# Self attention with exponentials summed on VectorE, products with ones a head group later, the next layernorm beside the maxima, and the query bias scaled later

## The chip, the cores and the metric

The kernel runs on one core of one Trainium2 chip. The core has five engines that run their own instruction queues side by side and wait for each other through semaphores: TensorE (PE in the profile, with its weight loads shown apart as PEld), VectorE (DVE), ScalarE (ACT), GpSimd (POOL) and SyncE (SP, which here only issues transfers). SBUF is the working memory of 128 partitions; PSUM takes what TensorE writes. The metric is the device time of one execution in microseconds (us). The time before is 848.01 us, the median of three runs (848.0 to 848.03).

## The reference

One decoder layer in float32 over four sequences (batches) of 512 tokens with 512 channels: self attention with 16 heads of 32 channels, cross attention against a given context, and a feed-forward part. Each begins with a layernorm and is added to x.

```python
x = x + attn(layernorm(x), q_w, q_b, k_w, k_b, v_w, v_b, o_w, o_b)   # causal, 16 heads of 32
x = x + xattn(layernorm(x), ctx, ctx)                                 # causal, 16 heads, masked by -10000
x = x + ffn(layernorm(x), W_up, W_down, W_gate, W_expert)

def attn(x, ...):
    q, k, v = x @ q_w.T + q_b, x @ k_w.T + k_b, x @ v_w.T + v_b      # split into heads
    scores = where(causal, einsum('bhqd,bhkd->bhqk', q, k) * 32 ** -0.5, -inf)
    ctx = einsum('bhqk,bhkd->bhqd', softmax(scores), v)
    return ctx @ o_w.T + o_b
```

What matters here is the softmax of the self attention: for every query, the largest score, the exponentials, their sum over the keys, and the quotient of the weighted values by that sum.

## The kernel before

**Stages.** Each of the four batches goes through the same stages (L781 to L824). with_maxima (L726) computes the scores with queries on the partitions and takes their largest values; between its matmuls it lays other matmuls as filler (query, key and value projections in the first batch, the feed-forward of the batch before later). attend (L753) computes the scores again with keys on the partitions, subtracts the maxima, takes exponentials and multiplies with the values. out_projection (L577) follows with the residual and the next layernorm; then the cross attention goes through the same two stages, and then the feed-forward. A group g is four heads on 128 partitions, so there are NC = 4 groups in a batch.

**Order.** The order of the instructions on PE, DVE, ACT and POOL is the order of the program text (manual_schedule, L773); SP's transfers are ordered by the framework. Every engine takes its queue in order, so an instruction that waits holds up everything behind it.

**PSUM.** All of PSUM is one pool of four buffers, each a pair of 512-column banks (pair, L65). A score unit takes two pairs (heads 0 and 1, heads 2 and 3), a group's value products one (pv: the numerators in half 0, the denominators in half 1).

**Attention stage, in steps.** attend goes through 12 units: for each group key block 0 (512 queries), key block 1 (384), and key blocks 2 and 3 together (256 and 128).
- scores (L360): eight matmul records per key block for the scores (L370; a float32 product is two records), then a bf16 product with ones that adds the negative maximum (L381). Two ScalarE exponentials (L394), each over a pair of heads, write pt in SBUF; two GpSimd selects (L396) set the masked corner to zero. pt lies in work buffers with the tags pt0, pt1 and pt2, two of each.
- values (L409) of a unit comes two units later: for u = 0 the products of pt with the values, for u = 1 those of pt with a matrix of ones (L418), which sum the exponentials over the keys and put the denominators into the second half of pv.
- divide (L429), after a group's last unit: VectorE transposes the denominators in 32x32 blocks (L438), takes the reciprocal of one column of each block (L440), transposes it back spread out (L441), and multiplies the numerators (L449) into oT, the tile that out_projection reads.
- The next batch's first layernorm (layernorms, L188, in five steps) is handed to attend as sides (L790) and runs on VectorE and GpSimd after every second unit; each of its first four steps also issues a transfer of 128 rows of x into xin (L466), which has two buffers. Its transposes (turns) run in out_projection.

**Maxima stage.** maxima (L267) takes per unit two pairs, two ScalarE copies into SBUF (L292), two GpSimd selects (L298) and VectorE reductions (L310). split (L323) makes three bf16 parts of a group's maxima, and rows (L334) transposes them on TensorE some units later.

**Start.** bqs_sb, the query bias times 1/sqrt(32), is made by a GpSimd instruction in the section of constants (L125). GpSimd's part in the layernorm, variance plus epsilon (L201) and its power -1/2 (L203), is in the same queue; VectorE normalizes with it (L209), TensorE transposes (L250), and the first projections (half, L518) follow.

Of the kernel before, what the change touches and what calls it, by code (L numbers as in the profile page):

```python
# [9 lines left out]
F32 = mybir.dt.float32  # L10
# [8 lines left out]
P = 128  # L19
# [7 lines left out]
def decoder_layer(  # L27
# [96 lines left out]
    bqs_sb = const.tile([P, NC], F32, name="bqs_sb")  # L124
    nc.gpsimd.tensor_scalar(bqs_sb, bq_sb, SCALE, None, ALU.mult)  # L125

# [134 lines left out]
    class Attention:  # L261
        def __init__(self, q_t, k_t, v, cross, name):
            self.q_t, self.k_t, self.v, self.cross, self.name = q_t, k_t, v, cross, name
            self.nm, self.mrow, self.pv, self.out = {}, {}, {}, None
            self.more, self.e = {}, None

# [93 lines left out]
        def scores(self, g, blocks):  # L360
# [17 lines left out]
            for j in blocks:  # L378
                for r in range(HG):
# [8 lines left out]
                    )  # L388
            pts = []
            for n in range(2):  # L390

                W = N if len(blocks) == 1 else S
                pt = work.tile([P, 2, W], F32, tag=f"pt{blocks[0]}", name=f"pt_{name}_{n}")
                nc.scalar.activation(pt[:, :, :N], scs[n][:, :, :N], AF.Exp)  # L394
                diagonal = pt.rearrange("p u (k q) -> p (u k) q", k=len(blocks))[:, :, :P]
                nc.gpsimd.affine_select(  # L396
                    out=diagonal,
                    in_=diagonal,
                    compare_op=ALU.is_ge,
                    fill=0.0,  # L400
                    base=0,
                    pattern=[[0, 2 * len(blocks)], [1, P]],
                    channel_multiplier=-1,
                )
                pts.append(pt)
            return pts

        def values(self, g, blocks, pts):

# [3 lines left out]
            at = {j: sum(S - k * P for k in blocks if k < j) for j in blocks}  # L413
            for u in range(2):
                for j in blocks:
                    for r in range(HG):
# [6 lines left out]
                            stop=(j == NT - 1),  # L423
                        )
            if blocks[-1] == NT - 1:
                self.divide(g)

        def divide(self, g):
            pv, name = self.pv.pop(g), f"{self.name}_{g}"  # L429
            num, den = pv[:, 0, :], pv[:, 1, :]  # L430
            if self.cross:
                beh, count = self.more.pop(g)
                nc.vector.tensor_tensor(count, den, count, ALU.add)
                nc.vector.tensor_tensor(beh, num, beh, ALU.add)
                num, den = beh, count

# [7 lines left out]
            )  # L444
            if self.cross:
                self.out = self.e.beh_t
            elif g == 0:
                self.out = act.tile([P, NC, S], F32, tag="o_t", name=f"oT_{self.name}")
            nc.vector.tensor_tensor(self.out[:, g, :], num, den_t, ALU.mult)  # L449
# [5 lines left out]
    def norm_in(b, given=None):  # L455

        e = Entry()
        e.b, e.x = b, given
        e.xn_t = act.tile([P, NC, S], F32, tag="xn_t", name=f"xnT_{b}")
        src = x[b].rearrange("(t p) d -> p t d", p=P)  # L460
# [9 lines left out]

        def turn(t):
            columns(
                [made[t], made[t + 1]],
                e.xn_t,
                t,
                pair(f"tp_a{b}_{t}"),
                warm=0 if b else 2,
            )
# [98 lines left out]
    def out_projection(e, a, sides):  # L577
# [3 lines left out]
        for c in range(NC):  # L581
            for t in range(NT):
# [5 lines left out]
                    stop=(c == NC - 1),  # L588
                )
            if c < NC - 1:  # L590
                run(sides[c::3])
# [133 lines left out]

    def with_maxima(steps, a, first=0):  # L726


        run(steps[:first])
        fill = matmuls(steps[first:])  # L730
# [4 lines left out]
        for n, (g, i) in enumerate(units):  # L735
            new = a.maxima(g, i)
            if i[-1] == NT - 1 and g > 0:
                jobs = a.rows(g - 1) + jobs
# [13 lines left out]

    def attend(a, late, sides=()):  # L753

        units = [(g, j) for g in range(NC) for j in ((0,), (1,), (2, 3))]
        waiting, sides = [], list(sides)
        for n, (g, j) in enumerate(units):
            waiting.append((g, j, a.scores(g, j)))
            if n == 4:
                run(a.rows(late))  # L760
            if len(waiting) > 2:
                a.values(*waiting.pop(0))
# [4 lines left out]
            if sides and n % 2 == 1:  # L767
                run([sides.pop(0)])
        while waiting:
            a.values(*waiting.pop(0))  # L770
        run(sides)
# [101 lines left out]
```

## Time and profile before

One profiled execution took 846.85 us, of which 844.8 us are the span from the first to the last instruction of the profile; the median of the unprofiled runs is 848.01 us.

| engine | busy us | share of the span | instructions |
|---|---|---|---|
| TensorE matmul | 824.7 | 98% | 6088 |
| TensorE weight load | 374.3 | 44% | 6088 |
| VectorE | 498.4 | 59% | 885 |
| ScalarE | 388.2 | 46% | 482 |
| GpSimd | 264.4 | 31% | 537 |

The stages that the change touches, first batch:

| stretch, us | what runs | TensorE busy | VectorE | ScalarE | GpSimd |
|---|---|---|---|---|---|
| 10 to 15 | layernorm at the start | 0.78 | 0.81 | 0.29 | 1.94 |
| 15 to 20 | first projections | 5.00 | 0.08 | 1.01 | 1.19 |
| 26 to 74 | maxima, projections | 48.00 | 26.82 | 23.28 | 11.58 |
| 72 to 107.6 | attention | 35.34 | 18.75 | 20.05 | 15.65 |

How to read such a profile: the shares tell which engine has least room, but only over the whole span; the chain that ended last follows the last instruction back through what released each step and so tells what set the time. A group line gives line, engine, operation, written and read tiles, shape and count, then busy time and mean duration in ns, then the idle time of the engine before these instructions and what ended it. A timeline line gives start and duration in us and, in brackets, the idle time before and its releaser. TensorE's matmuls are pipelined and their ends are modelled, so two groups' busy times may overlap; the distance between starts is the safer price. The granted TensorE clock is 1.00 in nearly all stretches; from 10 to 15 us it was 0.91 and from 15 to 20 us 0.75.

### The profile page before, as it was taken

How to read it: one execution, taken by the hardware profiler on the slowest of the kernel's cores; microseconds unless marked ns; L12 is line 12 of the kernel's file. 1: busy time of each engine (PE TensorE's matmuls, PEld its weight loads, DVE VectorE, ACT ScalarE, POOL GpSimd, SP SyncE). 2: the span in 40 equal slices, each digit the busy share in tenths (PEclk: the TensorE clock that was granted, in tenths of full speed). 3: DMA queues.
4: the chain of work that ended last, by engine and by line, in shares of the span. 5: the costliest groups of instructions: out<-in, count | busy, mean ns of one | idle time of the engine just before them, and what ended most of it. 6: DMA issues, size and time to landing. Idle time of an engine off the chain costs nothing.

```text
span 844.8 us, 14956 instructions
## 1 busy us (share of the span) xinstructions
PE 824.7 (98%) x6088; PEld 374.3 (44%) x6088; DVE 498.4 (59%) x885; ACT 388.2 (46%) x482; POOL 264.4 (31%) x537
## 2 busy tenths in 40 slices
PE   7999999999999999999999999999998999999998
PEld 6443454344443454444544445434443454344443
DVE  2446525967658424678756643596779325887511
ACT  1455615673355623556154551576256624565110
POOL 4323403342323522224322361234233333343100
PEclk9999999999999999999999999999999999999999
DMA  9500100001000100011100000000101100000101
GB/s 337 211 2 14 40 0 1 1 3 51 1 0 2 52 1 1 0 60 42 52 1 1 14 14 1 1 1 2 51 2 62 40 1 1 2 1 2 50 0 50
DMA packets 13541, 24.58 MB, mean 29 GB/s; under 512 B 1952, under 2 KB 1952, under 8 KB 13472
## 3 DMA queue, kind: packets, MB, share of 16 engines
q1 hardware_dynamic: 13184, 23.09, 8.1%
q8 instruction: 48, 0.79, 0.4%
q10 hardware_dynamic: 288, 0.52, 0.2%
q14 instruction: 21, 0.17, 0.1%
HBM read 19.42 MB, written 4.19 MB: 28 GB/s over the span
## 4 chain that ended last, share of the span: by engine, by line
PE 93%; ACT 3%; DVE 2%; DMA 1%; issue 1%; POOL 0%; SPq 0%; ACTq 0%
PE pm_qk L234 13%; PE pv_c L418 9%; PE pv_s L418 9%; PE pm_u L234 7%; PE pm_d L222 7%; PE pm_v L222 7%; PE pm_o L583 7%; PE pm_e L222 6%; PE sm_c L280 5%; PE sc_s L370 5%; PE sc_c L370 5%; PE sm_s L280 4%; DVE nm_s L310 1%; PE sc_s L381 1%; PE sc_c L381 1%; PE pm_qk L518 1%
## 5 line engine op out<-in xcount | busy, mean ns | idle before, releaser
L310 DVE TENSOR_REDUCE nm_c<-s_c 128x2 f32<-128x256 f32 (+3 forms) x128 | 96.3, 810 | 36.4 <-POOL s_c L298 36.4
L310 DVE TENSOR_REDUCE nm_s<-s_s 128x2 f32<-128x256 f32 (+3 forms) x128 | 96.7, 810 | 34.7 <-POOL s_s L298 34.7
L292 ACT COPY s_s<-sm_s 128x768 f32<-128x768 f32 (+1 forms) x96 | 78.9, 875 | 68.3 <-PE sm_s L280 50.3
L292 ACT COPY s_c<-sm_c 128x768 f32<-128x768 f32 (+1 forms) x96 | 78.9, 874 | 48.8 <-PE sm_c L280 34.6
L394 ACT ACTIVATE pt_s<-sc_s 128x768 f32<-128x768 f32 (+1 forms) x96 | 78.7, 884 | 47.8 <-PE sc_s L381 33.6
L394 ACT ACTIVATE pt_c<-sc_c 128x768 f32<-128x768 f32 (+1 forms) x96 | 78.6, 884 | 30.6 <-PE sc_c L381 25.9
L298 POOL TENSOR_SCALAR_AFFINE_SELECT s_s<-s_s 128x256 f32<-128x256 f32 (+1 forms) x96 | 46.3, 482 | 133.8 <-ACT s_s L292 132.8
L298 POOL TENSOR_SCALAR_AFFINE_SELECT s_c<-s_c 128x256 f32<-128x256 f32 (+1 forms) x96 | 46.5, 484 | 119.1 <-ACT s_c L292 118.0
L396 POOL TENSOR_SCALAR_AFFINE_SELECT pt_c<-pt_c 128x256 f32<-128x256 f32 (+1 forms) x96 | 56.4, 595 | 71.1 <-ACT pt_c L394 70.2
L396 POOL TENSOR_SCALAR_AFFINE_SELECT pt_s<-pt_s 128x256 f32<-128x256 f32 (+1 forms) x96 | 47.0, 494 | 57.4 <-ACT pt_s L394 56.5
L222 PE MATMUL pm_d<-wdown_sb,hT 128*128 128x512 f32 x128 | 60.4, 607 | 0.0
L222 PE MATMUL pm_e<-wexp_sb,fT 128*128 128x512 f32 x128 | 60.2, 605 | 0.0
L234 PE MATMUL pm_u<-fT,wup_sb 128*128 128x512 f32 x128 | 59.9, 608 | 0.0
L234 PE MATMUL pm_qk<-xnT,wk_sb 128*128 128x512 f32 x120 | 58.6, 610 | 0.0
L583 PE MATMUL pm_o<-wo_sb,oT_s 128*128 128x512 f32 x128 | 57.8, 596 | 0.0
L234 PE MATMUL pm_qk<-xnT,wq_sb 128*128 128x512 f32 x120 | 57.5, 606 | 0.0
L222 PE MATMUL pm_v<-wv_sb,xnT 128*128 128x512 f32 x128 | 57.4, 597 | 0.0
L370 PE MATMUL sc_s<-qT,kT 32*128 32x128 f32 (+3 forms) x512 | 51.8, 467 | 1.0 <-ACT pt_s L394 0.9
L370 PE MATMUL sc_c<-cqT,ckT 32*128 32x128 f32 (+3 forms) x512 | 51.9, 467 | 0.9 <-ACT pt_c L394 0.9
L280 PE MATMUL sm_c<-ckT,cqT 32*128 32x512 f32 (+3 forms) x512 | 49.1, 467 | 1.0 <-ACT cqT L258 1.0
L280 PE MATMUL sm_s<-kT,qT 32*128 32x512 f32 (+3 forms) x512 | 48.1, 467 | 1.4 <-ACT qT L503 1.4
L418 PE MATMUL pv_c<-pt_c,cv 128*32 128x128 f32 (+3 forms) x512 | 44.3, 441 | 0.0
(134 smaller groups left out, 1107.4 us busy)
## 6 DMA issues: line engine op xcount, KB each, us to landing
cv<-in_ctx_dram SPq DMA_DIRECT2D x16, 256.0 KB, 3.7
out_dram<-x SPq DMA_DIRECT2D x16, 256.0 KB, 2.0
x<-in_x_dram SPq DMA_DIRECT2D x14, 256.0 KB, 4.1
xin<-in_x_dram SPq DMA_DIRECT2D x12, 256.0 KB, 2.7
wq_sb<-in_wq_dram SPq DMA_DIRECT2D x2, 512.0 KB, 6.5
wk_sb<-in_wk_dram SPq DMA_DIRECT2D x2, 512.0 KB, 8.0
wv_sb<-in_wv_dram SPq DMA_DIRECT2D x1, 1024.0 KB, 8.3
wo_sb<-in_wo_dram SPq DMA_DIRECT2D x1, 1024.0 KB, 8.7
```

Of the source, the lines that this page charges most:

```text
L222: nc.tensor.matmul(pm, lhsT=lhs_t[:, c, t * P : (t + 1) * P], rhs=w[:, c, :], start=(c == 0), stop=(c == NC - 1),)
L234: nc.tensor.matmul(pm, lhsT=w[:, c, f * P : (f + 1) * P], rhs=rhs_t[:, c, :], start=(c == 0), stop=(c == NC - 1),)
L280: nc.tensor.matmul(scs[r // 2][:, r % 2, at[i] : at[i] + (i + 1) * P], lhsT=self.q_t[h, g, i * P : (i + 1) * P], rhs=self.k_t[h, g, : (i + ...
L292: nc.scalar.copy(s[:, :, :N], scs[n][:, :, :N])
L298: nc.gpsimd.affine_select(out=diagonal, in_=diagonal, compare_op=ALU.is_ge, fill=NEG, base=0, pattern=[[0, 2 * len(blocks)], [-1, P]], cha ...
L310: nc.vector.tensor_reduce(self.nm[g][:, i, 2 * n : 2 * n + 2], made[n][:, :, at[i] : at[i] + (i + 1) * P], axis=AX.X, op=ALU.max, negate=True,
L370: nc.tensor.matmul(scs[r // 2][:, r % 2, at[j] : at[j] + S - j * P], lhsT=self.k_t[h, g, j * P : (j + 1) * P], rhs=self.q_t[h, g, j * P :] ...
L381: nc.tensor.matmul(scs[r // 2][:, r % 2, at[j] : at[j] + S - j * P], lhsT=onesb[h, :], rhs=self.mrow[g][h, j * P :], start=False, stop=Tru ...
L394: nc.scalar.activation(pt[:, :, :N], scs[n][:, :, :N], AF.Exp)
L396: nc.gpsimd.affine_select(out=diagonal, in_=diagonal, compare_op=ALU.is_ge, fill=0.0, base=0, pattern=[[0, 2 * len(blocks)], [1, P]], chan ...
L418: nc.tensor.matmul(pv[r * HD : (r + 1) * HD, u, j * P :], lhsT=ones if u else self.v[:, j, h * HD : (h + 1) * HD], rhs=pts[r // 2][:, r % ...
L583: nc.tensor.matmul(pms[t // 2][:, t % 2, :], lhsT=a.out[:, c, t * P : (t + 1) * P], rhs=wo_sb[:, c, :], start=(c == 0), stop=(c == NC - 1),)
```

## The change

In self attention alone (the cross attention keeps its way):
- The exponentials of key block 0 are written into a larger tile, sums, in place of pt; it lies in the buffers of ck_t and beh_t by turns, which otherwise hold the context of the cross attention. After the products of a unit VectorE adds the next unit's exponentials into sums in place (add_up), six adds a group.
- values multiplies with the values only. The four products of sums with ones (summed) are issued one group later, into the second half of the next group's pv, after its block 0. The last group's are issued in out_projection after its first quarter, into a pair of their own (last_sum).
- At the end of a group ScalarE copies the numerators out of PSUM into oT; the denominators of the group before are transposed, inverted and spread by VectorE as before (spread), and GpSimd multiplies oT in place.

And besides:
- norm_in of the next batch is called before with_maxima, which appends one step of its layernorm to the VectorE work of every second unit; the tile xn_t is allocated later, at its first transposes.
- bqs_sb is scaled after the first layernorm and its transposes instead of among the constants.
- In the first batch three steps (skip) run before the first maxima instead of two: the two halves of the first query and key projection, and the next query projection.

```diff
     bqs_sb = const.tile([P, NC], F32, name="bqs_sb")
-    nc.gpsimd.tensor_scalar(bqs_sb, bq_sb, SCALE, None, ALU.mult)
...
             pts = []
+            if blocks[0] == 0 and not self.cross:
+                self.sums[g] = act.tile(
+                    [P, 2, 2, S], F32, tag=("ck_t", "beh_t")[g % 2], name=f"sum_{name}"
+                )
             for n in range(2):
                 W = N if len(blocks) == 1 else S
-                pt = work.tile([P, 2, W], F32, tag=f"pt{blocks[0]}", name=f"pt_{name}_{n}")
+                if blocks[0] == 0 and not self.cross:
+                    pt = self.sums[g][:, n]
+                else:
+                    pt = work.tile([P, 2, W], F32, tag=f"pt{blocks[0]}", name=f"pt_{name}_{n}")
                 nc.scalar.activation(pt[:, :, :N], scs[n][:, :, :N], AF.Exp)
...
-            for u in range(2):
+            for u in range(2 if self.cross else 1):
...
+            if self.cross:
+                if blocks[-1] == NT - 1:
+                    self.divide(g)
+                return
+            if blocks[0] == 0 and g > 0:
+                self.summed(g - 1, pv)
             if blocks[-1] == NT - 1:
-                self.divide(g)
+                if g == 0:
+                    self.out = act.tile([P, NC, S], F32, tag="o_t", name=f"oT_{self.name}")
+                nc.scalar.copy(self.out[:, g, :], pv[:, 0, :])
+                if g > 0:
+                    self.spread(g - 1, pv)
+
+        def add_up(self, g, blocks, pts):
+            at = {j: sum(S - k * P for k in blocks if k < j) for j in blocks}
+            for n in range(2):
+                for j in blocks:
+                    to = self.sums[g][:, n, :, j * P :]
+                    nc.vector.tensor_tensor(
+                        to, to, pts[n][:, :, at[j] : at[j] + S - j * P], ALU.add
+                    )
+
+        def summed(self, g, pv):
+            for r in range(HG):
+                nc.tensor.matmul(
+                    pv[r * HD : (r + 1) * HD, 1, :],
+                    lhsT=ones,
+                    rhs=self.sums[g][:, r // 2, r % 2, :],
+                    start=True,
+                    stop=True,
+                )
+
+        def spread(self, g, pv):
+            name = f"{self.name}_{g}"
+            den_t = work.tile([P, S], F32, tag="den_t", name=f"dt_{name}", bufs=1)
+            nc.vector.transpose(den_t, pv[:, 1, :])
+            rden = small.tile([P, S // HD, 1], F32, tag="rden", name=f"rden_{name}")
+            nc.vector.reciprocal(rden, den_t.rearrange("p (b d) -> p b d", d=HD)[:, :, 0:1])
+            nc.vector.transpose(
+                den_t.rearrange("p (b d) -> p b d", d=HD),
+                rden.to_broadcast([P, S // HD, HD]),
+            )
+            nc.gpsimd.tensor_tensor(self.out[:, g, :], self.out[:, g, :], den_t, ALU.mult)
+
+        def last_sum(self):
+            pv = pair(f"ls_{self.name}")
+            self.summed(NC - 1, pv)
+            self.spread(NC - 1, pv)
...
+            if c == 0:
+                a.last_sum()
             if c < NC - 1:
                 run(sides[c::3])
...
             new = a.maxima(g, i)
+            if norms and n % 2 == 0:
+                new.append(norms.pop(0))
...
-    def attend(a, late, sides=()):
+    def attend(a, late):
...
+        def values():
+            g, j, pts = waiting.pop(0)
+            a.values(g, j, pts)
+            if not a.cross and j != (2, 3):
+                a.add_up(*waiting[0])
...
         run(turns)
+        nc.gpsimd.tensor_scalar(bqs_sb, bq_sb, SCALE, None, ALU.mult)
         add_bias(e)
         between_self = query_key(e) + value(e)
-        skip, between_cross, ahead = 2, [], []
+        skip, between_cross, ahead = 3, [], []
...
-            late = with_maxima(between_self, sa, skip)
-            if b == B - 1:
-                e.x = load_x(b)
             norms, turns = [], []
             if more:
                 after, norms, turns = norm_in(b + 1)
-            attend(sa, late, norms)
+            late = with_maxima(between_self, sa, skip, norms)
+            if b == B - 1:
+                e.x = load_x(b)
+            attend(sa, late)
```

More of the change, by code (lines that the diff above doesn't have):

```diff
@@ L264, in __init__ @@
             self.nm, self.mrow, self.pv, self.out = {}, {}, {}, None
-            self.more, self.e = {}, None
+            self.more, self.sums, self.e = {}, {}, None
         def maxima(self, g, blocks):
@@ L406, in scores, with values @@
             return pts
-        def values(self, g, blocks, pts):
+        def values(self, g, blocks, pts, later=None):
             if blocks[0] == 0:
@@ L430, in divide @@
             num, den = pv[:, 0, :], pv[:, 1, :]
[L431 to L435, printed above, removed]
+            beh, count = self.more.pop(g)
+            nc.vector.tensor_tensor(count, den, count, ALU.add)
+            nc.vector.tensor_tensor(beh, num, beh, ALU.add)
+            num, den = beh, count
             den_t = work.tile([P, S], F32, tag="den_t", name=f"dt_{name}", bufs=1)
@@ L444, in divide @@
             )
[L445 to L448, printed above, removed]
+            self.out = self.e.beh_t
             nc.vector.tensor_tensor(self.out[:, g, :], num, den_t, ALU.mult)
@@ L457, in norm_in @@
         e = Entry()
-        e.b, e.x = b, given
-        e.xn_t = act.tile([P, NC, S], F32, tag="xn_t", name=f"xnT_{b}")
+        e.b, e.x, e.xn_t = b, given, None
         src = x[b].rearrange("(t p) d -> p t d", p=P)
@@ L471, in turn @@
         def turn(t):
+            if e.xn_t is None:
+                e.xn_t = act.tile([P, NC, S], F32, tag="xn_t", name=f"xnT_{b}")
             columns(
@@ L724, in matmuls, with with_maxima @@
             yield
-    def with_maxima(steps, a, first=0):
+    def with_maxima(steps, a, first=0, norms=()):
+        norms = list(norms)
         run(steps[:first])
@@ L751, in with_maxima @@
         return NC - 1
-    def attend(a, late, sides=()):
+    def attend(a, late):
         units = [(g, j) for g in range(NC) for j in ((0,), (1,), (2, 3))]
-        waiting, sides = [], list(sides)
+        waiting = []
+        def values():
[3 more added lines that the diff above has]
+                a.add_up(*waiting[0])
         for n, (g, j) in enumerate(units):
@@ L761, in attend @@
             if len(waiting) > 2:
-                a.values(*waiting.pop(0))
+                values()
             if a.cross and j == (0,):
@@ L766, in attend @@
                 a.masked(g)
-            if sides and n % 2 == 1:
-                run([sides.pop(0)])
         while waiting:
-            a.values(*waiting.pop(0))
-        run(sides)
+            values()
     with tc.manual_schedule(engines=BY_HAND):
```

## The prediction, made before the changed kernel ran

> **What bounds it now.** I read the shares by engine, the chain that ended last, the groups by shape, and the timeline of the stages that the change touches. First the page:
>
> ```profile
> span 844.8 us, 14956 instructions
> PE 824.7 (98%) x6088; PEld 374.3 (44%) x6088; DVE 498.4 (59%) x885; ACT 388.2 (46%) x482; POOL 264.4 (31%) x537
> PE 93%; ACT 3%; DVE 2%; DMA 1%; issue 1%; POOL 0%; SPq 0%; ACTq 0%
> ```
>
> The chain is TensorE nearly throughout: work taken from it should come off the end, as long as nobody else is late. So each step asks what TensorE saves and who is late next. The products with ones, grouped by shape (busy, mean ns):
>
> ```profile
> L418 PE MATMUL pv_s<-pt_s,ones 128*32 128x512 f32 x128 | 16.7, 592 | 0.0
> L418 PE MATMUL pv_s<-pt_s,ones 128*32 128x384 f32 x128 | 13.3, 486 | 0.0
> L418 PE MATMUL pv_s<-pt_s,ones 128*32 128x256 f32 x128 | 9.8, 379 | 0.0
> L418 PE MATMUL pv_s<-pt_s,ones 128*32 128x128 f32 x128 | 6.4, 273 | 0.0
> ```
>
> Every product is two records. Busy times overlap at their ends, so I price by starts. Two parts of the timeline, a middle head group and the start (start, duration, engine, line; in brackets the idle time and its releaser):
>
> ```profile
> 88.87 0.31 PEld L370 LDWEIGHTS sc_s<-qT,kT 32*128 32x128 f32 x8 [0.84 <-issue]
> 90.16 0.85 PE L418 MATMUL pv_s<-pt_s,v 128*32 128x384 f32 x8
> 90.32 1.94 ACT L394 ACTIVATE pt_s<-sc_s 128x1024 f32<-128x1024 f32 x2 [1.63 <-PE sc_s L381]
> 90.83 0.83 PE L418 MATMUL pv_s<-pt_s,ones 128*32 128x384 f32 x8
> 91.59 0.31 PEld L370 LDWEIGHTS sc_s<-qT,kT 32*128 32x128 f32 x8 [0.62 <-ACT pt_s L394]
> 92.76 1.51 ACT L394 ACTIVATE pt_s<-sc_s 128x768 f32<-128x768 f32 x2 [0.51 <-POOL pt_s L396]
> 94.05 0.74 PEld L370 LDWEIGHTS sc_s<-qT,kT 32*128 32x128 f32 x16 [0.20 <-issue]
> ```
>
> ```profile
> 12.30 0.24 POOL L125 TENSOR_SCALAR bqs_sb<-bq_sb 128x4 f32<-128x4 f32 x1 [4.61 <-DMA bq_sb<-in_bq_dram]
> 14.22 1.09 PE L250 MATMUL tp_a<-ident,xn_a 128*128 128x128 f32 x4 [4.54 <-DVE xn_a L209]
> 25.58 0.54 PEld L280 LDWEIGHTS sm_s<-kT,qT 32*128 32x128 f32 x16 [1.76 <-ACT qT L503]
> ```
>
> Call S0, S1, S23 a group's three score units and V0, V1, V23 their value products. Scores start at 88.87, 91.59 and 94.05, the next group at 96.93: 8.06 us a group, TensorE without a gap. The line at 91.59 matters most: S1 was released by the first exponential of S0 (90.32 plus 1.02, at 91.34). There are four PSUM pairs: one holds pv, two hold S0, so S1 needs a pair that this exponential frees.
>
> **Start: bqs_sb.** GpSimd stands behind the query bias (4.61 us) and keeps back two reciprocal deviations, and TensorE stands 4.54 us. Moved behind them, the third block goes: statistics end at 9.34, its normal (0.55) at 9.9, transposes from 9.98; the fourth's GpSimd work (0.22 and 0.57, after 9.42) ends at 10.35, normal 10.95, transposes 11.05, the first projections at 11.5 instead of 16.81: 5.3. The first eight took 2.07 us from start to start at a granted clock of 0.75 (the window 15 to 20), the next eight 1.73: 0.3 more. The weights allow it: wq landed at 9.11, wk at 11.87 (needed at 13.2), the biases at 12.23. The third projection (skip 3) now covers the copies of q and k, the 1.36 us that TensorE stood before 25.58. Sum **7.0**; bounds 5.5 (a late normal) and 7.2.
>
> **Norms beside the maxima.** Five steps of some 1.5 us of VectorE, no TensorE work. Between 26 and 74 us VectorE was busy 26.8 of 48, between 220 and 267 28.4 of 47; the last batch, where L310 does hold TensorE, has no norms. The DMA of xin moves with them. In the first batch xin landed at 31.67 behind the weights in SP's queue; its statistics now stand behind unit 0's reductions (28.09 to 30.0 before, 3.6 earlier now) and hold VectorE some 5 us. Behind them the reductions of units 1 and 2 and the split end at 31.67 + 0.9 + 1.9 + 2.4 + 0.9 = 37.8; the row transposes that need them stood at 45.90 and come at about 41. Later batches: SP's transfers before xin are cv's, issued by 205 us, long before that stage at 221. Cost 0; without that slack of 3 us the rest of the delay is paid. Out of the attention stage go VectorE's 6 us a batch; TensorE did not wait for these.
>
> **Attention, TensorE.** By starts, ones cost 0.86 (512), 0.64 (384), 0.64 (256 and 128) a group; 0.86 comes back as the later product. V1 and V23 fall from 1.43 to 0.79, V0 stays 1.85. Taken alone: 8.06 to 6.77.
>
> **What is late next.** S1 could start at S0 + 1.29 + 0.79 = 2.08, but S0's exponential starts 1.45 after S0, takes 1.02 and frees the pair at 2.53 with 0.06 for the signal: stall 0.45. S23 needs S1's first exponential: 1.17 + 0.815 + 0.06 = S1 + 2.04, against 1.02 + 0.79 = 1.81: stall 0.23. Then S23 1.03 and V0 1.85: 2.53 + 2.04 + 2.88 = 7.45. ScalarE's new copy (0.69, as L500's 691 ns) fits between the second pair of exponentials (S1 + 2.68) and S23's, which start 0.14 later; the pair they free is wanted only 0.7 us after that. So a group gains **0.61**, not 1.29.
>
> Per batch: the first value products save 0.86, of which 0.60 counts (the fifth of the six exponentials started at 75.63 frees the pair); group 1 gains 0.83 (its row transposes, 0.33, use up S23's stall); groups 2 and 3 0.61 each; V1 and V23 at the end 1.29. Against: last_sum is eight records (0.86) and two changes of tiling (0.12 each, as between V1 and S1): 1.1. And the last V23 wants its selects: they ended 2.37 after V0's start (105.50 after 103.13), now 2.5 with the copy, and it comes at 2.55; two 768-element adds start at 1.05 and hold them back by 0 to 1.5; I take 1.1, as both adds run then. Sum 0.60 + 0.83 + 1.22 + 1.29 - 1.1 - 1.1 = **1.7**, four batches **7.0**. The PSUM pair of last_sum leaves one for the two transposes behind it: 0 to 1.2 us in three batches; 0, since VectorE's first transpose (0.72) frees it before the second comes.
>
> **VectorE and GpSimd.** The trace has no add of 768 elements out of SBUF; nearest are L310's reductions of the same lengths (943, 675, 411 ns) and L357 (706 at 512). Two of each: 4.06 a group, 3.8 back to back, 4.7 at most if each is stretched like L449 behT (794 to 691). With two transposes and a reciprocal, 1.68, VectorE has 5.5 of 7.45. The sums lie in buffers that only the cross stage uses. An add of block 1 waits for V0's reads; behind it stand the adds of S23 and spread, read by TensorE one group later, with some 2.3 us to spare. GpSimd: selects 4 x 0.406 and 2 x 0.67, product 1.27 (L484): 4.2 a group. Do they exclude each other? In the cross stage:
>
> ```profile
> 186.60 1.21 DVE L568 TENSOR_TENSOR_SCAN behT<-ckT,zero 128x511 f32<-128x511 f32 x1
> 195.28 1.11 POOL L396 TENSOR_SCALAR_AFFINE_SELECT pt_c<-pt_c 128x256 f32<-128x256 f32 x1 [2.34 <-ACT pt_c L394]
> ```
>
> A select of 0.41 takes 1.11 beside a scan, ending 0.2 after it: half of a select lies outside the exclusion. VectorE's cycle lies between 5.5 (never blocked) and 9.7 (blocked by all 4.2); I take 6.9, a third of it, and it is off the end up to about 8. The Trainium skill, "SBUF — State Buffer", section "Who interferes with whom", speaks against the change: a VectorE instruction with two SBUF inputs and a GpSimd instruction that reads SBUF lock each other out for the whole instruction. By it adds and GpSimd's work take 4.06 + 4.2 = 8.3 us a group, above the old 8.06, and the attention would gain nothing; the scan's row agrees that they exclude each other, not that it is for the whole.
>
> **Sum.** Against the profiled execution's own 846.85 us (span 844.8): 7.0 + 7.0 off gives 832.85. The median of the runs, 848.01, lies 1.16 above: **834**. Own range 829 to 838: 5.5 to 7.2 of the start and 1.0 to 3.0 a batch.
>
> **Rivals.** (B) The slots don't bind, because pairs come free in another order: per batch 0.86 + 4 x 1.29 - 1.1 = 4.9, so 848 - 7 - 19.7 = **821**. For it: TensorE heads the chain everywhere. Against it: the release at 91.59.
> (C) VectorE with GpSimd becomes the pace at the old 8.06 a group: the batch has 0.60 + 1.29 - 2.2 = -0.3, leaving the start: **842**. For it: 5.5 to 9.7 holds 8.06.
> (D) Slower: the same exclusion at some 9.2 a group, adds always behind selects and product. Three groups in each of four batches, 12 x 1.14 = 13.7, with C's 1.2 less the start's 7: **856**. It decides from 8.06 + 5.8 / 12 = 8.54 a group; against it the 2.3 us of slack and only four groups a batch.
> That the change misses its aim at the start (xn's late normal comes from elsewhere) would add 7 to each; the releaser named leaves it little.
>
> **Chances.** Forecast 0.55, B 0.19, C 0.18, D 0.08. Differences of under 0.2% (1.7 us) can't be told from none here: faster 0.90 (all but an edge of C, and D), same 0.03, slower 0.07. The range of 8 in 10 takes half of B and most of C: 824 to 842.
>
> **What would show it.** Right: transposes of the first batch without a gap, maxima from about 22 us; S1's weight load behind ACT pt_s with TensorE idle 0.3 to 0.5 us; 7.3 to 7.6 us a group; last_sum without a wait. Wrong: products of sums waiting for VectorE (C, D), selects of well over 1 us in the middle groups (D), groups of 6.8 (B), L310 or parts holding TensorE beside the maxima (norms not free).

## The result and the profile after

The changed kernel took **853.46 us** (median of four runs, 850.8 to 854.84) against 848.0 (846.4 to 848.03) for the kernel before on the same chip: a ratio of 1.0065, 95% interval 1.0036 to 1.0094. The forecast was 834.0 with a range up to 842; it was wrong in size and in sign. The profiled execution took 850.8 us. Three executions further below (one each of the kernel before, of the product on VectorE and of the kernel without adds) took 1328 to 1372 us at a granted clock of 0.56; all medians and ratios here go by the other, fast ones.

The experiments were timed in two groups, each with the kernel before beside it: its medians were 847.09 and 847.18 us there, and 848.0 here. So a difference between the changed kernel's median and that of an experiment carries about 1 us from that, besides the changed kernel's own spread.

The page of the changed kernel, with the lines that answer to those of before:

```profile
span 849.1 us, 14293 instructions
...
PE 819.7 (97%) x5704; PEld 368.2 (43%) x5704; DVE 567.3 (67%) x965; ACT 396.6 (47%) x498; POOL 307.4 (36%) x553
...
PE 85%; DVE 7%; POOL 3%; ACT 3%; issue 2%; DMA 0%; ACTq 0%
```

384 matmul records are gone, and TensorE's busy time fell by only 5 us. Its part of the chain fell from 93 to 85%, and VectorE and GpSimd now stand in the chain with 7 and 3% (2 and 0 before). The shares alone don't say who is late: the fastest kernel below has the same 85 and 7%, and only GpSimd's part is gone there. The question is where TensorE waits.

**The start** did what was forecast. Timeline of the changed kernel (start, duration, engine, line, shapes, count, and in brackets the idle time before with its releaser):

```profile
9.86 0.63 PE L249 MATMUL tp_a<-ident,xn_a 128*128 128x128 f32 x4 [0.29 <-DVE xn_a L208]
...
11.55 1.89 PE L572 MATMUL pm_qk<-xnT,wq_sb 128*128 128x256 f32 x8
...
12.02 0.24 POOL L841 TENSOR_SCALAR bqs_sb<-bq_sb 128x4 f32<-128x4 f32 x1 [1.60 <-DMA bq_sb<-in_bq_dram]
...
21.98 0.54 PEld L279 LDWEIGHTS sm_s<-kT,qT 32*128 32x128 f32 x16 [0.76 <-issue]
```

The 4.54 us of idle time at the transposes are 0.29, the first projections start at 11.55 (16.81 before), the first maxima at 21.99 (25.58). The attention of the first batch starts at 67.00 instead of 74.19: 7.2 us earlier.

**The attention** gives it back. This table is read from the starts of the score units and of the first out product (pm_o) in the timelines. Group 0 is S0 of group 0 to S0 of group 1, and so on; the end is S0 of group 3 to the first out product; "out" is the first to the last of the four quarters of out_projection.

| batches 0 / 1 / 2 / 3, us | group 0 | group 1 | group 2 | group 3 and end | attention | out |
|---|---|---|---|---|---|---|
| before, each | 6.29 | 8.39 | 8.06 | 10.65 | 33.38 | 13.90 (batch 3: 8.72, counted to the third) |
| the prediction, each | 5.69 | 7.56 | 7.45 | 9.85 | 30.55 | 15.0 |
| after | 5.38 | 8.62 / 8.62 / 8.61 / 9.48 | 7.17 | 13.35 / 12.69 / 13.34 / 13.35 | 34.52 / 33.86 / 34.51 / 35.39 | 15.58 / 15.16 / 15.74 / 10.46 |

The middle groups are faster than forecast; group 1 and the end of each batch are slower than before. The list of TensorE's waits (total us, how often, longest) has two new lines:

```profile
PE pv_s L427 <- POOL pt_s L403: 12.0, 4, 3.0
PE sc_s L369 <- DVE mrow_s L343: 2.7, 4, 1.3
```

The first is the last V23 of each batch, the second the scores in group 1. The end of the first batch in the timeline of the kernel before:

```profile
104.16 1.34 POOL L396 TENSOR_SCALAR_AFFINE_SELECT pt_s<-pt_s 128x512 f32<-128x512 f32 x2 [1.36 <-ACT pt_s L394]
...
106.16 0.83 PE L418 MATMUL pv_s<-pt_s,v 128*32 128x256 f32 x16
...
107.58 1.98 PE L583 MATMUL pm_o<-wo_sb,oT_s 128*128 128x512 f32 x4
```

There GpSimd stood ready for the exponential, its selects were done at 105.50, and V23 followed without a wait. The same place in the changed kernel:

```profile
95.48 0.71 DVE L474 STREAM_TRANSPOSE dt_s<-rden_s 128x512 f32<-128x512 f32 x1
95.69 0.83 PE L427 MATMUL pv_s<-pt_s,v 128*32 128x384 f32 x8
...
96.11 2.85 DVE L452 TENSOR_TENSOR sum_s<-sum_s,pt_s 128x768 f32<-128x768 f32 x2
96.27 1.88 POOL L478 TENSOR_TENSOR oT_s<-oT_s,dt_s 128x512 f32<-128x512 f32 x1 [1.48 <-DVE dt_s L474]
...
98.11 1.94 POOL L403 TENSOR_SCALAR_AFFINE_SELECT pt_s<-pt_s 128x512 f32<-128x512 f32 x2
99.50 2.62 DVE L452 TENSOR_TENSOR sum_s<-sum_s,pt_s 128x512 f32<-128x512 f32 x4 [0.53 <-POOL pt_s L403]
...
99.52 2.08 PE L427 MATMUL pv_s<-pt_s,v 128*32 128x256 f32 x16 [3.00 <-POOL pt_s L403]
...
101.53 4.13 PE L637 MATMUL pm_o<-wo_sb,oT_s 128*128 128x512 f32 x8
```

Read from the bottom: the last V23 waited 3.00 us for a select that began at 98.11. Its exponentials were ready long before (the first at 94.90), but in GpSimd's queue the product L478 stands ahead of the selects, and the product waited until 96.19 for VectorE's spread-out denominators and then ran 1.88 us beside two adds. These denominators in turn stood behind the adds of the unit before, and those adds behind that unit's selects, which stood behind the product before. One turn of this ring lasts from one product to the next, 88.30 to 96.27, so 8.0 us.

Behind the batch's first product, at 88.30, the same order cost TensorE only 0.48 us: S0 and S1 of group 3 lie between the exponentials of group 2 and its V23. The selects ended at 91.51 and 92.09, V23 began at 91.65 without idle time, and S1 to S23 took 2.67 us in group 3 against 2.19 in group 2. At the end of a batch no scores lie between, and V23 was wanted at 96.52.

### The profile page after: what moved, and what is told of

It reads as the page before. It is cut to its first block, busy times and chain, and to the rows that moved or that the text cites. A ratio compares the mean times of both kernels' runs of the same rounds, so it can differ in the third digit from the quotient of the medians.

```text
span 849.1 us, 14293 instructions
## 1 busy us (share of the span) xinstructions
PE 819.7 (97%) x5704; PEld 368.2 (43%) x5704; DVE 567.3 (67%) x965; ACT 396.6 (47%) x498; POOL 307.4 (36%) x553
## 4 chain that ended last, share of the span: by engine, by line
PE 85%; DVE 7%; POOL 3%; ACT 3%; issue 2%; DMA 0%; ACTq 0%
PE pm_qk L233 13%; PE pv_c L427 9%; PE pm_u L233 7%; PE pm_d L221 7%; PE pm_o L637 7%; PE pm_v L221 7%; PE pm_e L221 6%; PE sm_c L279 5%; PE sc_c L369 5%; PE sm_s L279 4%; PE sc_s L369 3%; DVE sum_s L452 3%; PE pv_s L427 3%; POOL oT_s L478 2%; POOL pt_s L403 1%
## 5 line engine op out<-in xcount | busy, mean ns | idle before, releaser
L309 DVE TENSOR_REDUCE nm_c<-s_c 128x2 f32<-128x256 f32 (+3 forms) x128 | 96.3, 810 | 36.6 <-POOL s_c L297 36.6
L309 DVE TENSOR_REDUCE nm_s<-s_s 128x2 f32<-128x256 f32 (+3 forms) x128 | 96.6, 810 | 27.8 <-POOL s_s L297 27.8
L452 DVE TENSOR_TENSOR sum_s<-sum_s,pt_s 128x512 f32<-128x512 f32 (+1 forms) x96 | 84.2, 910 | 14.4 <-PE pv_s L427 9.0
L369 PE MATMUL sc_s<-qT,kT 32*128 32x128 f32 (+3 forms) x512 | 59.2, 468 | 3.6 <-DVE mrow_s L343 2.7
L401 ACT ACTIVATE pt_s<-sc_s 128x768 f32<-128x768 f32 x64 | 48.1, 814 | 10.1 <-issue 4.4
```

The costliest lines, as they stand in the source:

```text
L309: nc.vector.tensor_reduce(self.nm[g][:, i, 2 * n : 2 * n + 2], made[n][:, :, at[i] : at[i] + (i + 1) * P], axis=AX.X, op=ALU.max, negate=True,
L369: nc.tensor.matmul(scs[r // 2][:, r % 2, at[j] : at[j] + S - j * P], lhsT=self.k_t[h, g, j * P : (j + 1) * P], rhs=self.q_t[h, g, j * P :] ...
L452: nc.vector.tensor_tensor(to, to, pts[n][:, :, at[j] : at[j] + S - j * P], ALU.add)
```

## The experiments

Theory R (ring): GpSimd's product in front of the selects, in two in-order queues that wait for each other, holds the end of each batch; the mutual slowing of VectorE's adds and GpSimd's work makes the ring too long. Rivals: the part at the start or the norms did not bring what was reckoned; the busy time of VectorE alone is the pace; the PSUM pairs are.

**One part alone: the start.** The kernel before with bqs_sb moved and skip 3:

```diff
-    nc.gpsimd.tensor_scalar(bqs_sb, bq_sb, SCALE, None, ALU.mult)
...
         run(turns)
+        nc.gpsimd.tensor_scalar(bqs_sb, bq_sb, SCALE, None, ALU.mult)
...
-        skip, between_cross, ahead = 2, [], []
+        skip, between_cross, ahead = 3, [], []
```

> The kernel before with the query bias scaled behind the first layernorm and three steps ahead of the maxima, nothing else. All theories: the profile of the change shows the first scores of the attention stage 7.19 us earlier (67.00 against 74.19), so 848.0 - 7.2 = 840.8 us, and the stages behind as before. A time over 843 would say that part of the loss lies outside the attention stage.

Measured: 839.63 us, ratio 0.9906 (0.9889 to 0.9923). The start is worth 7.5 us by the medians (847.09 before) and 7.2 by the timelines. So the rest of the change, forecast at 7.0 gained, costs 853.46 - 839.63 = 13.8 us.

**One part alone: the norms.** The kernel before with its next layernorm beside the maxima:

```diff
-            attend(sa, late, norms)
+            late = with_maxima(between_self, sa, skip, norms)
...
+            attend(sa, late)
```

> The kernel before with one part of the change alone: the five steps of the next batch's layernorm moved from the attention to the maxima. The prediction's term was a cost of 0, and no gain either, since TensorE did not wait for these steps where they were: 847 to 849. Rival 1 (the steps late behind xin hold up the maxima or the row transposes): 2 us or more in batch 0, so 850 and above, with new waits on VectorE's L310 or the parts. Rival 2 (VectorE's steps did hold the old attention stage): 845 or less.

Measured: 846.6 us, ratio 0.9993 (0.9984 to 1.0003), and every column of the table as before to 0.01 us. The term of 0 holds for this part alone (0.6 us below the 847.18 of the kernel before, and 0.4 below the range expected). In the changed kernel the attention of the first batch starts at 67.00, with the start alone at 66.98: beside the other parts, too, the norms cost the first maxima nothing.

**The adds left out.**

```diff
             a.values(g, j, pts)
-            if not a.cross and j != (2, 3):
-                a.add_up(*waiting[0])
```

> The changed kernel without VectorE's adds; the sums then hold the first key block alone. All theories: no wait for selects at the end, clock 1.0. What it tells is the pace of TensorE when nothing else is late: by the prediction's PSUM reckoning 7.45 us a group (the first unit to the next group's first), about 830 us; if the pairs do not bind, 6.8 us a group and 821 us.

Measured: 833.89 us, ratio 0.9839 (0.9822 to 0.9855). Group 1 takes 7.47 and group 2 7.23, close to the forecast's 7.56 and 7.45: TensorE's side of the reckoning was about right, and the PSUM pairs do bind. The adds cost 853.46 - 833.89 = 19.6 us. But even here the last V23 waits 1.4 us a batch for selects behind the product, where no wait was expected, so the order of GpSimd's queue costs something without any add.

**The same length of work without the second SBUF input.** Each add becomes a reduction of the same exponentials, with the same waits and in the same place:

```diff
-                    nc.vector.tensor_tensor(
-                        to, to, pts[n][:, :, at[j] : at[j] + S - j * P], ALU.add
-                    )
+                    nc.vector.tensor_reduce(
+                        to[:, :, 0:1],
+                        pts[n][:, :, at[j] : at[j] + S - j * P],
+                        AX.X,
+                        ALU.add,
+                    )
```

> The changed kernel with each add replaced by a reduction of the same exponentials, which reads one tensor of SBUF and writes one column of the sum buffer, so that waits, order and VectorE's busy time nearly stay (943, 675 and 411 ns each); the sums of the other key blocks are left out of the result. Theory A, the ring over GpSimd's and VectorE's queues binds only because adds and GpSimd's work stretch each other: selects back at 0.41 and 0.67, the product at 1.27, the ring 1.27 + 1.34 + 2.17 + 1.68 = 6.5 and some 0.3 of signals, under 7.4; groups 1 to 2 of 7.2 to 7.6, a wait of 1 to 1.6 at the end of each batch as without any adds, in all 833 to 839. Theory B, the order of the queues and the number of VectorE's instructions alone: groups and waits as in the changed kernel, 850 to 855.

Measured: 834.43 us, ratio 0.9848 (0.9833 to 0.9863), as good as without any adds. The groups by shape (busy us, mean ns) of the changed kernel:

```profile
L452 DVE TENSOR_TENSOR sum_s<-sum_s,pt_s 128x768 f32<-128x768 f32 x32 | 43.3, 1391 | 9.1 <-PE pv_s L427 9.0
...
L403 POOL TENSOR_SCALAR_AFFINE_SELECT pt_s<-pt_s 128x512 f32<-128x512 f32 x32 | 29.9, 945 | 11.1 <-ACT pt_s L401 10.6
...
L452 DVE TENSOR_TENSOR sum_s<-sum_s,pt_s 128x512 f32<-128x512 f32 x32 | 26.7, 836 | 4.2 <-POOL pt_s L403 4.2
L478 POOL TENSOR_TENSOR oT_s<-oT_s,dt_s 128x512 f32<-128x512 f32 x16 | 25.2, 1575 | 32.7 <-DVE dt_s L474 32.7
...
L452 DVE TENSOR_TENSOR sum_s<-sum_s,pt_s 128x256 f32<-128x256 f32 x32 | 16.1, 502 | 1.1
```

And of the kernel with reductions:

```profile
L452 DVE TENSOR_REDUCE sum_s<-pt_s 128x2 f32<-128x768 f32 x32 | 28.7, 938 | 9.7 <-PE pv_s L427 9.6
...
L452 DVE TENSOR_REDUCE sum_s<-pt_s 128x2 f32<-128x512 f32 x32 | 21.8, 680 | 2.2 <-POOL pt_s L403 2.2
...
L481 POOL TENSOR_TENSOR oT_s<-oT_s,dt_s 128x512 f32<-128x512 f32 x16 | 20.3, 1267 | 31.5 <-DVE dt_s L477 31.5
L403 POOL TENSOR_SCALAR_AFFINE_SELECT pt_s<-pt_s 128x512 f32<-128x512 f32 x32 | 20.0, 637 | 7.9 <-ACT pt_s L401 7.5
```

With one SBUF input on VectorE every row has its undisturbed duration on both engines: reductions 938 ns, product 1267, selects 637. With two, the same rows are 1391, 1575 and 945. The shortest adds of the changed kernel took 0.92, 0.68 and 0.42 us, as long as the reductions, so the adds aren't longer work by themselves. A reduction also writes fewer columns; that this isn't the difference shows at 94.45 in the changed kernel, where a transpose out of PSUM that writes 512 columns of SBUF took its 0.70 us while a GpSimd select ran on to 94.80. So it isn't VectorE's amount of work but that its adds and GpSimd's instructions keep each other waiting. One pair shows how, at the start of the turn of the ring read above: the product stood from 88.30 to 90.20 and the second add from 88.98 to 91.01, the first add from 88.14 to 89.06. The product got its turn when the first add was done (1.14 us before its own end), the second add when the product was done (0.81 before its own). This pair takes turns by whole instructions, with an overlap of about 0.1 us.

The Trainium skill, "SBUF — State Buffer", section "Who interferes with whom", states that a VectorE instruction with two SBUF inputs contends with a GpSimd instruction that reads SBUF. It says of VectorE's two-port modes that whoever issues first gets the ports for the whole instruction, and of a reduction that it never contends on trn2. The rows agree with the first and the last, and the pair above shows whole instructions for adds, too.

**The order alone.** The product is issued behind the next unit's selects; adds and their slowing stay:

```diff
-            nc.gpsimd.tensor_tensor(self.out[:, g, :], self.out[:, g, :], den_t, ALU.mult)
+            self.last = lambda: nc.gpsimd.tensor_tensor(self.out[:, g, :], self.out[:, g, :], den_t, ALU.mult)
...
             waiting.append((g, j, a.scores(g, j)))
+            a.quotient()
```

(quotient issues what stands in self.last; it is also called at the ends of attend and last_sum.)

> The changed kernel with the GpSimd product issued behind the selects of the unit that follows, the same instructions in another order. Ring theory: selects of the third unit no longer wait for the product, last wait 1.2 us or less, clock 1.0, 838 to 844 us. Port theory and VectorE theory: the same work on the same engines, 851 to 855 us, the wait stays at 2 to 3 us.

Measured: 839.21 us, ratio 0.9898 (0.9883 to 0.9912): 14.2 us for one instruction moved in one queue. The end of the first batch in its timeline:

```profile
94.37 1.34 POOL L404 TENSOR_SCALAR_AFFINE_SELECT pt_s<-pt_s 128x512 f32<-128x512 f32 x2 [0.66 <-ACT pt_s L402]
...
95.12 1.49 PE L428 MATMUL pv_s<-pt_s,v 128*32 128x384 f32 x24
95.58 5.00 DVE L453 TENSOR_TENSOR sum_s<-sum_s,pt_s 128x768 f32<-128x768 f32 x6
95.74 1.91 POOL L479 TENSOR_TENSOR oT_s<-oT_s,dt_s 128x512 f32<-128x512 f32 x1
...
96.53 3.70 PE L644 MATMUL pm_o<-wo_sb,oT_s 128*128 128x512 f32 x8
```

The selects follow the exponential, V1 and V23 run without a gap, and the out products start 8.48 us after S0 of group 3 instead of 13.35. The adds and the product still stretch each other (5.00 us for six adds, 1.91 for the product), but nobody on TensorE waits for them there. This parts the end of a batch into its causes: 13.35 us in the changed kernel, 10.57 with reductions (the order stays, the exclusion is gone), 8.48 here (the exclusion stays, the order is gone). So 2.1 us are the order alone and 2.8 more (2.1 in batch 1, where the clock stayed) come when the exclusion stretches what stands ahead of the selects; without that order the exclusion costs the end nothing. Part of what was won is lost a little later. TensorE's waits:

```profile
PE tp_a L249 <- DVE dt_s L472: 5.0, 3, 1.7
PE sc_s L370 <- DVE mrow_s L344: 2.7, 4, 1.3
```

With the end earlier, last_sum meets its adds still running, and its PSUM pair is missing to the side transposes: out_projection takes 17.40 instead of 15.2 to 15.7.

**The product on VectorE**, out of GpSimd's queue altogether:

```diff
-            nc.gpsimd.tensor_tensor(self.out[:, g, :], self.out[:, g, :], den_t, ALU.mult)
+            nc.vector.tensor_tensor(self.out[:, g, :], self.out[:, g, :], den_t, ALU.mult)
```

> The changed kernel with the product of numerators and quotients on VectorE instead of GpSimd. Ring theory (the GpSimd product stands ahead of the selects of the third unit, VectorE's adds wait for these, spread for the adds, and the product for spread; the end of this ring is the loss): the last value products wait 1.2 us or less instead of 3.0, TensorE's clock stays at 1.0 in all batches, 840 to 845 us. Theory that VectorE has simply too much work there: it gets 16 x 0.7 = 11 us more, 855 us or more. Theory that the port between VectorE and GpSimd is the pace wherever the work stands: about 1 of 6 us of port time moves, 848 to 852 us.

Measured: 848.10 us, ratio 1.0011 (1.0001 to 1.002): outside what theory R expected, and inside the 848 to 852 of the port theory named there. The attention does as R says, 29.65 us a batch (30.52 in the last). But from batch 1 on out_projection takes 20.55, 21.58 and 14.01. The timeline of batch 1 tells why:

```profile
286.50 7.25 POOL L538 TENSOR_TENSOR x<-x,bo_sb 128x512 f32<-128x512 f32 x4
287.00 8.10 DVE L452 TENSOR_TENSOR sum_s<-sum_s,pt_s 128x768 f32<-128x768 f32 x6
...
294.18 2.89 PE L458 MATMUL ls_s<-sum_s,ones 128*32 128x512 f32 x8 [3.12 <-DVE sum_s L452]
```

With GpSimd free earlier, the addition of the output bias to x (add_bias, from batch 1 on in GpSimd's queue behind the attention) starts beside the last adds. Its four instructions of 1.27 us take 7.25 and the six adds, 3.94 in batch 0 without that neighbour, 8.10; last_sum waits 3.12 for them. The same exclusion with other partners: an engine that became free sooner started work that collided. So the port theory is right in that the exclusion can move with the work; the run before this one, where 851 to 855 was its forecast and 839.21 was measured, shows that it isn't the pace wherever the work stands.

**What the wait costs besides its length.** In the changed kernel the granted clock fell behind the wait. Its windows in the first batch (stretch; length, then busy time and count of each engine; granted clock; DMA share; GB/s):

```profile
core 0: us, PE busy (x) PEld busy (x) DVE busy (x) ACT busy (x) POOL busy (x), PEclk, DMA share, GB/s
96.00:98.00 2.00, 0.52 (x8) 0.00 (x0) 2.00 (x3) 0.00 (x0) 1.73 (x1) 1.00 0.00 0
98.00:100.00 2.00, 0.48 (x4) 0.19 (x4) 1.47 (x2) 0.00 (x0) 2.00 (x3) 0.75 0.00 0
100.00:102.00 2.00, 2.00 (x17) 1.19 (x14) 1.93 (x4) 0.36 (x1) 0.05 (x1) 0.50 0.00 0
102.00:104.00 2.00, 2.00 (x5) 0.79 (x5) 1.78 (x4) 0.23 (x1) 0.00 (x0) 0.89 0.00 0
```

The experiment lays ten small products without use into that wait:

```diff
         while waiting:
+            if not a.cross and len(waiting) == 1:
+                keep_warm(f"warm_{a.name}", 10)
             values()
```

> The changed kernel with ten small products without use (some 2.3 us at the full clock) in TensorE's queue just ahead of the last V23 of each self attention, where it waits 3.0 us for selects. The theory that the wait costs twice, once as idle time and once by the halved clock behind it: the selects end when they did, the last V23 takes 0.65 instead of 2.0 us and the first out products 3.53 instead of 4.06, in three batches: 5 to 6 us less, 847 to 849, and no clock below 0.9 in that place. Rival (the lower clock comes from what the later work draws, not from the idle time): the dips stay, 852 to 855.

Measured: 847.27 us, ratio 1.0006 (0.9997 to 1.0016), 6.2 us less than the changed kernel with more work on TensorE. Its timeline:

```profile
96.15 2.50 PE L182 MATMUL warm_s<-ident 128*128 128x128 f32 x20
97.81 1.94 POOL L403 TENSOR_SCALAR_AFFINE_SELECT pt_s<-pt_s 128x512 f32<-128x512 f32 x2
...
99.22 1.43 PE L427 MATMUL pv_s<-pt_s,v 128*32 128x256 f32 x16 [0.57 <-POOL pt_s L403]
100.58 3.70 PE L637 MATMUL pm_o<-wo_sb,oT_s 128*128 128x512 f32 x8
```

The selects come when they did, the clock is 1.00 throughout this place, and V23 takes 1.36 us from start to start instead of 2.01 (not the 0.65 expected: its second half still waits for the second select, until 99.75). So the wait's own length is one loss and the lower clock behind it a second, of some 6 us over a run by the medians. (The profiled execution, 848.72, has one fall of the clock elsewhere, which the last section takes up.)

**Both kernels beaten.** The later product, and the two waits left in it removed: the last group's row transposes one unit earlier, so that their copy stands ahead of the adds on VectorE, and last_sum behind the first side transposes:

```diff
-            if n == 4:
+            if n == (4 if a.cross else 3):
                 run(a.rows(late))
...
-            if c == 0:
-                a.last_sum()
             if c < NC - 1:
                 run(sides[c::3])
+            if c == 0:
+                a.last_sum()
```

> The kernel with the later product (839.2) and two more moves: the row transposes of the last group one unit earlier, so that their copy stands ahead of the adds in VectorE's queue, and last_sum behind the first side transposes. What waits is left in its trace: 2.7 us at mrow (0.7 a batch), 5.0 at the second side transposes (three batches), 1.3 at last_sum. Theory: these are separate waits and all go: 839.2 - 2.7 - 5.0 - 1.3 = 830; 829 to 834. Rival: the PSUM pairs only pass the wait on to the next that needs a pair: 836 to 840.

Measured: **829.28 us** (829.19 to 829.45), ratio 0.9787 (0.9773 to 0.9802). Group 1 takes 7.96 (8.83 in batch 3), the attention 29.0, out_projection 15.47. Its waits at the two places:

```profile
PE tp_a L249 <- DVE dt_s L472: 0.5, 3, 0.2
...
PE sc_s L370 <- DVE mrow_s L344: 0.2, 1, 0.2
```

The two waits were separate and went; only some 0.5 us came back, as TensorE now waits 2.4 instead of 1.9 us for the row parts (in batch 3, 0.44 us at 640.82). With the start alone at 839.63, the rebuilt attention is worth 10.4 us once its queues are in the right order.

## Why the prediction was wrong, step by step

The profiled executions differ from the forecast by 850.8 - 832.85 = 17.95 us. The table above places it: the end of the batches 13.3 (3 x 3.50 + 2.84), group 1 5.1 (3 x 1.06 + 1.92), out_projection 2.1, less 2.3 that groups 0 and 2 were better and 0.2 of the start.

- **Start, 7.0.** Right: 7.2 in the timeline, 7.5 by the run of this part alone, with the terms where they were put (5.3 before the projections, the rest before the maxima).
- **Norms beside the maxima, 0.** Right; measured alone, 846.6 against 847.18.
- **Group of 7.45 because of the PSUM pairs.** Nearly right: 7.17. S0 to S1 takes 2.06 us, not 2.53. I read the release at 91.59 as holding all of S1; after the change S1's first products started at 83.08 while only those from 83.47 waited for the exponential that ended at 83.42, so half of S1 covers the stall. S1 to S23 takes 2.19 (forecast 2.04), S23 to the next S0 2.92 (2.88).
- **"The last V23 wants its selects ... I take 1.1".** This is the step that failed. It reckoned when the exponentials allow the selects and how far adds hold them back, but not what stands ahead of them in GpSimd's queue: the product, which waits for VectorE's transposes. The product was in the sum of GpSimd's load (4.2 of 7.45 us, room enough), and a load says nothing on order. The wait was 3.0 us in each batch instead of 1.1, V23 behind it took 1.36 instead of 0.65 because its second half waits for the second select, and in three of four batches the clock fell in addition. One product moved in the queue gave 14.2 us.
- **VectorE's cycle, "3.8 back to back, 4.7 at most if each is stretched".** The bound was too low: 2 x 1.391 + 2 x 0.836 + 2 x 0.502 = 5.46 us of adds a group. But this is 1.4 us over six of the shortest (4.03), a third of GpSimd's 4.2, and with the 1.68 of transposes and reciprocal it makes 7.1 us a group: the 6.9 that I took was nearly right and is below the group's 7.17. The reason given for the third was not: a select ending soon after a scan (the scan beside that select began at 194.98; the row shown at 186.60 is its like in another group) tells of an overlap of 0.1 to 0.2 us, not of a share. So the size agrees by luck, and as load the exclusion was not mispriced. What it does is stretch the ring. That the ring's 8.0 us come near the 8.3 worked out in the prediction is no proof of that sum: they hold VectorE's transposes too, beside which GpSimd stood idle (1.48 us before the product).
- **Rivals C and D.** They had the exclusion, the right mechanism, but put it into the pace of all groups. The one group that pays for it there is group 1 (8.62 against 7.47 with reductions), through the copy of the next point; group 2 ran at 7.17, faster than forecast. That D came nearest in time (856) is luck: it has 9.2 us a group.
- **Group 1's row transposes, "0.33, use up S23's stall".** They take their 0.33, but I did not price the copy behind them. It stands on VectorE behind adds that wait for selects, and its PSUM tile holds a pair: scores in group 1 wait 2.7 us in all by TensorE's records. The group itself is 1.15 us longer than with reductions, as most of S23's products stand behind that wait (their weight loads waited 0.86 us in the first batch). With the copy one unit earlier 0.2 remain of the wait, and the group takes 7.96.
- **last_sum, 1.1; its pair, 0.** Right in the changed kernel (15.16 instead of 13.90 where the clock stayed up), but only since the end was late: with the product moved the pair cost 1.7 us in each of three batches.
- Of the signs for being wrong, one did show: a select of "well over 1 us in the middle groups", the sign of D. In 15 of 16 groups one of the two selects of 512 elements took 1.23 to 1.36 us. The others did not (products of sums waiting for VectorE, groups of 6.8, L309 holding TensorE). Of the signs for being right, the start and last_sum without a wait showed; the groups of 7.3 to 7.6 came out below. No sign stood for the wait for selects at the end of a batch.

The table and the runs agree on the causes of the miss; the run-to-run spread of the changed kernel (850.8 to 854.84) is taken up below.

## What to carry to other kernels

When an instruction is put on an engine that has room, walk its queue: what does the new instruction wait for, what stands behind it, and who waits for that; a ring over two in-order queues can be longer than either engine's load, and it shows where the other work that hides it ends, here at the end of a stage. Price VectorE instructions with two SBUF inputs and GpSimd instructions as taking turns, and look what else GpSimd starts when it becomes free. Where a TensorE wait can't be removed, work without use laid into it can keep the clock, which was worth 6 us here.

## What the runs showed of the hardware that was not expected

The half clock comes in pieces of one length, on a grid. In the changed kernel's profile the granted clock fell at 99.02, 501.79 and 682.70 us after the span's start, and each time it was back after 3.41 us. (In the kernel with the product on VectorE one fall, at 501.77, lasted 6.83 us, twice that, though TensorE was idle for only 0.85 us of its first half.) Counted from the first change to full clock at 6.86, the three times are 27, 145 and 198 times 3.4133 us, to 0.01 us; between the same grid lines, in the piece just before a fall, TensorE had been idle 2.50, 2.82 and 2.84 us. In batch 1 the same wait of 3.0 us lay across a grid line, 1.93 on one side and 1.06 on the other, and the clock stayed. So whether a wait of 2 to 3 us costs the clock depends on where it falls: that accounts for the shorter end of batch 1 (12.69 instead of 13.35) and fits the runs, whose time goes with the mean granted clock (850.8 at 0.994, 852.57 at 0.992, 854.35 and 854.84 at 0.989 and 0.990). In the runs with useless products the time was 847.04 to 847.34 at a mean clock of 1.000 and 848.72 to 849.13 at 0.998.

The Trainium skill, "TensorE: Matmul & The Clock Gate", section "What's actually happening", states a free-running window of 3413 ns, which these times agree with. Its section "HAM oscillation — how this bites in real kernels" gives the rule that no idle gap of TensorE should be over some 3.4 us; here 2.27 us idle in one window were enough (in the kernel with the product on VectorE, in the window that ended at 501.77), and 1.98 us in another were not (in the fastest kernel, in the window that ended at 825.46). One more fall is left open: in the profile with useless products the clock fell at 660.32 after only 1.33 us idle in its window, while the same wait in the changed kernel had no such effect.
